# Two residual additions moved from TensorE to VectorE in a graph attention kernel

## The chip, the cores and the metric

The kernel runs on one core of one Trainium2 chip. The metric is the device time of one execution in microseconds (us); lower is better. Three runs of the kernel before the change are given.

## The reference, cut to what matters

One graph attention layer with four heads, a residual and a layer norm. `x` is 4096x512, `adj` is 4096x4096, `W` is 512x2048, `a` is 4x1024x1, all in float32.

```python
ht = (h @ W).reshape(N, N_HEADS, N_HIDDEN).transpose(1, 0, 2)
src = jnp.einsum('hnd,hd->hn', ht, a[:, :N_HIDDEN, 0])
dst = jnp.einsum('hnd,hd->hn', ht, a[:, N_HIDDEN:, 0])
e = jax.nn.leaky_relu(src[:, :, None] + dst[:, None, :], SLOPE) + adj_mat[None]
att = jax.nn.softmax(e, axis=-1)
h_prime = jnp.einsum('hij,hjd->hid', att, ht).mean(axis=0)
x = _layernorm(x + h_prime, axis=-1)
```

The entries of `adj` reach 1e9 while the scores beside them are small. Where the largest entry of a row leads by enough, the softmax of that row is one-hot: the row's output is then `layernorm(x[i] + x[col] @ mean_over_heads(W))`, with `col` the column of the largest entry. The kernel computes that (`leading_rows`), tests at the end that every row leads by enough, and has a second function (`general`) for the rows that don't. With these inputs the second is not entered.

## The kernel before, in words

The 4096 rows are 32 blocks of 128. The main loop of `leading_rows` runs over t from 0 to 31, and the order of every engine's instructions is the order in which this Python code is written: nothing is rearranged, so each engine has one fixed list. At step t the code writes:

- SP: the load of `adj` of block t+5 (2 MB; six buffers, so the load waits until VectorE has finished with block t-1).
- VectorE: `segment_maxima(t)` reads the 128x4096 tile of `adj` and takes maxima of its segments (line 212; in one piece in blocks 12 to 19, in two halves before and after), `find_segment(t)` finds the row's largest segment (lines 222 and 224), and `find_column(t-2)` finds the largest entry in that segment of block t-2, which GpSimd has fetched again (lines 264 and 270). In blocks 5 to 19 `find_column` stands behind `find_segment`, from block 20 on between the halves of `segment_maxima`.
- GpSimd (POOL): from VectorE's index, the fetch of the segment (`lead`, line 230), and from the column the fetch of the row of `x` (`y`, line 255), both indirect DMAs of one row for each partition.
- TensorE (PE), for block t-3: `spread` (one matmul `px`, line 331), `turn` (four transposes of `y`, line 284), `residual` (the block of x, which lies in `hold`, times the identity, into the sum `o` in PSUM, line 296; a float32 matmul is two records in the profile), `from_table` (three bf16 matmuls, line 343) and `products` (`y` times the mean of W over the heads, four float32 matmuls in eight records, line 303).
- ScalarE (ACT): `off` and `pick` from `px` (lines 333 and 335), the copy of the transposes to SBUF (`yt`, line 286), then for block t-4 `row_norm` (the sum of squares of x, which reads `hold`, line 347) and `parked_stats` (lines 372 and 374: it copies the sum `o` from PSUM over x in `hold` and takes mean and variance), and for block t-11 `finish` (line 391), and `clear_rows` for the next gather (line 245).

`root` (line 377) takes the square roots of the deviations of four blocks at once, 12 to 15 at t = 19 and 16 to 19 at t = 23. `add_sums` (line 360) exists already for two of the last blocks: VectorE adds the sum in PSUM and x.

```python
def residual(ib):
    start = ib not in o_ps
    if start:
        o_ps[ib] = psum.tile([P, D], F32, name="o")
    nc.tensor.matmul(o_ps[ib], ident, hold[:, ib, :], start=start, stop=False)

def add_sums(ib, out):
    nc.vector.tensor_add(out, o_ps[ib], hold[:, ib, :])
    o_ps[ib] = out
```

Of the kernel before, what the change touches and what calls it, by code (L numbers as in the profile page):

```python
# [27 lines left out]
LAST = 4  # L28
SKIP = 8192
TABLED = range(1, 28)  # L30


@with_exitstack
# [40 lines left out]
def leading_rows(ctx, tc, x, adj, W, a, out, ident, leads, any_bad):  # L74
# [17 lines left out]
    BEHIND = LATE - Q  # L92
# [3 lines left out]
    hold = landing.tile([P, NB, D], F32, name="hold")  # L96
# [22 lines left out]
    def pieces(ib):  # L119
        return PIECES if ib == NB - 1 else 2 if ib >= LATE else 1  # L120

    def load_adj(ib):
        if 0 <= ib < NB:
            t = adj_t[ib] = adj_pool.tile([P, N], F32, name="adj_t")
            n = pieces(ib)
            for k in range(n):
                rows_of = adj_rows[ib - 1] if ib else adj[:P, :]
                nc.sync.dma_start(t[:, ts(k, N // n)], rows_of[:, ts(k, N // n)])

    def load_x(lo, n):  # L130
        if lo == 0:
            nc.sync.dma_start(hold[:, 0, :], x[:P, :])
            lo, n = 1, n - 1
        if n:
            nc.sync.dma_start(hold[:, ds(lo, n), :], x_rows[:, ds(lo - 1, n), :])
# [59 lines left out]
    def span_of(ib):  # L195
        return next(k for k, (_, lo, hi) in enumerate(spans) if lo <= ib < hi)
# [4 lines left out]
    def segment_maxima(ib, lo, hi):  # L201

        if ib == NB - 1:
            for k in range(lo, hi):
                nc.vector.max(out=best[:, k, :], in_=adj_t[ib][:, ts(k, N // PIECES)])
            return
        e = spans[span_of(ib)][0]
        if lo == 0:
            seg_of[ib] = small.tile([P, N // e], F32, name=f"seg{e}", bufs=2)
        n = max(pieces(ib), 1 if ib in WHOLE else 2)  # L210
        for k in range(lo * n // PIECES, hi * n // PIECES):
            nc.vector.tensor_reduce(  # L212
                seg_of[ib][:, ts(k, N // e // n)],
                adj_t[ib][:, ts(k, N // n)].rearrange("p (s e) -> p s e", e=e), axis=AX.X, op=OP.max,
            )

    def find_segment(ib):
        if ib == NB - 1:
            nc.vector.max(out=top[:, ib, :], in_=best)
            return  # L220
        seg = seg_of.pop(ib)
        nc.vector.max(out=top[:, ib, :], in_=seg)  # L222
        at = at_of[ib] = small.tile([P, 8], U32, name="at")
        nc.vector.max_index(at, top[:, ib, :], seg)  # L224
        row = small.tile([P, 1], U32, name="row")
        nc.gpsimd.tensor_tensor(row, at[:, 0:1], first[:, ib : ib + 1], op=OP.add)  # L226
        k = span_of(ib)
        e = spans[k][0]
        lead = lead_pool.tile([P, e], F32, name=f"lead{e}", bufs=LEADS[k])
        nc.gpsimd.indirect_dma_start(  # L230
            out=lead, out_offset=None, in_=adj_segs[e],
            in_offset=bass.IndirectOffsetOnAxis(ap=row[:, :1], axis=0),
        )
        lead_of[ib] = lead
        start = at_of[ib] = small.tile([P, 1], U32, name="start")
        if ib in TABLED:
            away = small.tile([P, 1], F32, name="away")
            nc.gpsimd.tensor_scalar(away, at[:, 0:1], float(P // e), float(SKIP), op0=OP.is_lt, op1=OP.mult)
            nc.gpsimd.tensor_scalar(start, at[:, 0:1], float(e), away, op0=OP.mult, op1=OP.add)
        else:  # L240
            nc.gpsimd.tensor_tensor(start, at[:, 0:1], width[:, k : k + 1], op=OP.mult)
# [5 lines left out]
    def gather_rows(ib, col):  # L247
        if ib not in TABLED:
            y = y_t[ib] = y_pool.tile([P, D], F32, name="y")
            nc.gpsimd.indirect_dma_start(  # L250
                out=y, out_offset=None, in_=x,
                in_offset=bass.IndirectOffsetOnAxis(ap=col[:, :1], axis=0),
            )
            return
        nc.gpsimd.indirect_dma_start(  # L255
            out=y_t[ib], out_offset=None, in_=x,
            in_offset=bass.IndirectOffsetOnAxis(ap=col[:, :1], axis=0),
            bounds_check=N - 1, oob_is_err=False,
        )
        low = low_of[ib] = small.tile([P, 1], BF16, name="low")  # L260
        nc.gpsimd.tensor_scalar(low, col, float(SKIP - 1), float(SKIP - 1), op0=OP.max, op1=OP.subtract)
# [4 lines left out]
    def find_column(ib):  # L266
        if ib < BEHIND:
            find_inner(ib)
        within = small.tile([P, 8], U32, name="within")
        nc.vector.max_index(within, top[:, ib, :], lead_of[ib])  # L270
        col = small.tile([P, 1], U32, name="col")
        nc.gpsimd.tensor_tensor(col, at_of.pop(ib), within[:, 0:1], op=OP.add)  # L272
        gather_rows(ib, col)
# [15 lines left out]
    def turn(ib):  # L289
        yt_of[ib] = turned_rows(y_t.pop(ib))  # L290
# [68 lines left out]
# [3 lines that stand above are left out]
# [8 lines left out]
    def parked_stats(ib):  # L370
        o, i = o_ps.pop(ib), slice(ib, ib + 1)
        nc.scalar.activation(hold[:, ib, :], o, AF.Identity, scale=-1.0 / D, accum_out=nm[:, i])  # L372
        sq = rows.tile([P, D], F32, name="sq")
        nc.scalar.activation(sq, hold[:, ib, :], AF.Square, bias=nm[:, i], scale=-float(D), accum_out=sd[:, i])  # L374
# [4 lines left out]
    def scales(i):  # L379
        nc.gpsimd.tensor_mul(nm[:, i], nm[:, i], sd[:, i])  # L380
        nc.gpsimd.tensor_scalar(sd[:, i], sd[:, i], -float(D), None, op0=OP.mult)
# [153 lines left out]
    COLUMN, PROJECT, STATS = 2, 3, 4  # L535
# [4 lines left out]
    def lag_of(hi):  # L540
        return hi - 1 + STATS + (3 if hi < BEHIND - 2 else 2)
# [4 lines left out]
    for t in range(NB):  # L546
        if t == NB // 2:
            tc.mark_branch_hint_location("general", engines=HINTED)
        if t in x_at:
            load_x(*x_at[t])  # L550
        if t + AHEAD == NB - 1:
            load_x(LATE, 2)
        load_adj(t + AHEAD)
        middle = PIECES if t in END else 1 if t == NB - 1 else 2
        segment_maxima(t, 0, middle)
        if t >= COLUMN and t not in END and t != COLUMN + 1:
            find_column(t - COLUMN)
            if t == lag_of(BEHIND) + 1:
                scales(slice(BEHIND - 2, BEHIND))
        if t not in END:  # L560
            segment_maxima(t, middle, PIECES)
        if t == NB - 1:
            for ib in (BEHIND, LATE + 2, BEHIND + 2):
                load_x(ib, 2)
        find_segment(t)
        if t in END:
            find_column(t - 1 if t <= COLUMN else t - COLUMN)
        if t + 1 in TABLED:
            clear_rows(t + 1)
        for lo, hi in FACTORS:  # L570
            if t == lag_of(hi):
                nc.vector.reciprocal(sd[:, lo:hi], sd[:, lo:hi])
                if hi < BEHIND:
                    scales(slice(lo, hi))
        if t < 2:
            mean_of_heads(t)
        elif t == 2:
            mean_of_heads(2)
            mean_of_heads(3)
            fill_table()  # L580
        if t == 0:
            square_sums_of_a()
        if 21 <= t < 24:
            head_norms(t - 21)
        ib = t - PROJECT
        if t == NB - 2:
            finish(BEHIND - 3)
            finish(BEHIND - 2)
        if t == NB - 1:
            row_norm(LATE)  # L590
            row_norm(LATE + 1)
            finish(BEHIND - 1)
            residual(LATE + 1)
        if ib >= 0:
            if ib in TABLED:
                spread(ib)
            turn(ib)
            if ib > BEHIND:
                products(ib - 1, KB - 1, KB)
            if ib < BEHIND:  # L600
                residual(ib)
            if ib in TABLED:
                from_table(ib)
            products(ib, 0, KB if ib < BEHIND else KB - 1)
            if ib == 0:
                split_table()
        for _ in range(squares_at.get(t, 0)):
            square_sum_of_w(squares.pop(0))
        if t >= BEHIND + STATS:
            put_by(t - STATS)  # L610
        elif t >= STATS:
            row_norm(t - STATS)
            parked_stats(t - STATS)
        for lo, hi in FACTORS:
            if t == hi - 1 + STATS:
                root(slice(lo, hi))
        for done in FINISHED.get(t, ()):
            finish(done)
# [253 lines left out]
```

## Time and profile before

| | |
|---|---|
| median of three runs | 233.9 us (233.88 to 234.27) |
| profiled execution | 233.53 us, of which the span from the first to the last instruction is 232.0 us |
| PE busy | 197.6 us (85% of the span) |
| DVE (VectorE) busy | 189.6 us (82%) |
| ACT (ScalarE) busy | 153.2 us (66%) |
| POOL (GpSimd) busy | 111.5 us (48%) |
| DMA | 96.04 MB, mean 414 GB/s |

The busy shares are averages over stages with different limits. In the timeline a row is: start in us, duration in us, engine, line, operation, output tile from input tile, shapes, count, and in brackets the idle time of the engine before the row with what ended it. "Step t" below is the step of the main loop; because each engine has its own list, the engines are at different steps at one moment: TensorE's work of step t is on block t-3.

### The profile page before, as it was taken

How to read it: one execution, taken by the hardware profiler on the slowest of the kernel's cores; microseconds unless marked ns; L12 is line 12 of the kernel's file. 1: busy time of each engine (PE TensorE's matmuls, PEld its weight loads, DVE VectorE, ACT ScalarE, POOL GpSimd, SP SyncE). 2: the span in 40 equal slices, each digit the busy share in tenths (PEclk: the TensorE clock that was granted, in tenths of full speed). 3: DMA queues.
4: the chain of work that ended last, by engine and by line, in shares of the span. 5: the costliest groups of instructions: out<-in, count | busy, mean ns of one | idle time of the engine just before them, and what ended most of it. 6: DMA issues, size and time to landing. Idle time of an engine off the chain costs nothing.

```text
span 232.0 us, 2532 instructions
## 1 busy us (share of the span) xinstructions
PE 197.6 (85%) x604; PEld 95.5 (41%) x614; DVE 189.6 (82%) x296; ACT 153.2 (66%) x378; POOL 111.5 (48%) x254
## 2 busy tenths in 40 slices
PE   0069988779099999997999899999999999999990
PEld 0033443334044444443444345454544444545460
DVE  0448289899879997999699959996999999967882
ACT  3003213588075987797998678878888877958872
POOL 4020414525554556355635665554565665637620
PEclk9999999999859999999999999999999999999997
DMA  6999999999999999999999999999999999999995
GB/s 221 426 435 428 433 421 437 425 431 411 440 429 422 420 437 427 429 421 434 418 433 430 417 435 429 419 430 431 426 432 415 419 425 416 419 416 419 420 374 207
DMA packets 13379, 96.04 MB, mean 414 GB/s; under 512 B 2148, under 2 KB 2596, under 8 KB 7984
## 3 DMA queue, kind: packets, MB, share of 16 engines
q1 hardware_dynamic: 9792, 88.08, 90.0%
q0 software_dynamic: 3552, 7.73, 8.5%
q8 instruction: 6, 0.10, 0.2%
q14 instruction: 13, 0.11, 0.1%
q10 hardware_dynamic: 16, 0.02, 0.0%
HBM read 88.51 MB, written 8.39 MB: 418 GB/s over the span
## 4 chain that ended last, share of the span: by engine, by line
DMA 44%; PE 30%; DVE 19%; ACT 2%; issue 1%; POOL 1%; DVEq 0%; POOLq 0%; ACTq 0%
DMA adj_t<-in_adj_dram 39%; PE o L303 19%; DVE seg L212 15%; DMA y<-in_x_dram,col 4%; PE o L296 3%; PE o L343 3%; PE tp L284 3%; PE o L400 2%; DVE at L224 1%; DVE top L222 1%; DMA a_rows<-in_L_gnn_a_dram 1%; DVE inner L264 1%; POOL lead L230 0%; PE o L396 0%; ACT sq L368 0%
## 5 line engine op out<-in xcount | busy, mean ns | idle before, releaser
L212 DVE TENSOR_REDUCE seg<-adj_t 128x128 f32<-128x2048 f32 (+4 forms) x54 | 138.9, 2589 | 27.4 <-DMA adj_t<-in_adj_dram 27.4
L303 PE MATMUL o<-w_sum,yt 128*128 128x512 f32 x248 | 113.5, 598 | 1.1 <-ACT yt L286 0.8
L303 PEld LDWEIGHTS o<-w_sum,yt 128*128 128x128 f32 x248 | 46.8, 192 | 49.0 <-issue 42.0
L230 POOL DMA_INDIRECT lead<-in_adj_dram,row x31 | 32.5, 1050 | 14.5 <-POOL row L226 14.5
L255 POOL DMA_INDIRECT y<-in_x_dram,col x27 | 29.1, 1077 | 12.1 <-POOL col L272 6.1
L226 POOL TENSOR_TENSOR row<-at,first 128x1 uint32<-128x1 uint32 x31 | 5.8, 188 | 60.0 <-DVE at L224 43.6
L284 PE MATMUL tp<-ident,y 128*128 128x128 f32 x128 | 22.9, 302 | 12.0 <-DMA y<-in_x_dram,col 11.9
L286 ACT COPY yt<-tp 128x512 f32<-128x512 f32 x33 | 19.0, 576 | 14.2 <-PE tp L284 13.9
L451 PE MATMUL o<-hold,ident 128*128 128x512 f32 x32 | 16.4, 671 | 14.0 <-DMA hold<-in_L_gnn_W_dram 14.0
L284 PEld LDWEIGHTS tp<-ident,y 128*128 128x128 f32 x128 | 18.3, 210 | 23.9 <-issue 17.8
L296 PE MATMUL o<-hold,ident 128*128 128x512 f32 x50 | 26.5, 612 | 0.0
L333 ACT ACTIVATE off<-px,minus 128x128 f32<-128x128 f32 x27 | 9.9, 366 | 19.9 <-PE px L331 19.8
L343 PE MATMUL o<-z,pick 128*128 128x512 bf16 x72 | 20.4, 386 | 1.1 <-ACT pick L335 0.8
L347 ACT ACTIVATE sq<-hold 128x512 f32<-128x512 f32 x32 | 20.0, 625 | 0.0
L391 ACT ACTIVATE hold<-hold,nm,sd 128x512 f32<-128x512 f32 x24 | 18.8, 801 | 0.0
L374 ACT ACTIVATE sq<-hold,nm 128x512 f32<-128x512 f32 x24 | 17.3, 722 | 0.8
L452 ACT ACTIVATE w_sum<-o 128x512 f32<-128x512 f32 x4 | 2.4, 597 | 22.5 <-PE o L451 22.5
L245 ACT COPY y<-zero 128x512 f32<-128x512 f32 x27 | 16.3, 603 | 0.0
L451 PEld LDWEIGHTS o<-hold,ident 128*128 128x128 f32 x32 | 6.7, 216 | 22.9 <-issue 21.6
L343 PEld LDWEIGHTS <-pick 128*128 128x128 bf16 x81 | 7.8, 100 | 19.9 <-issue 10.5
L372 ACT ACTIVATE hold<-o 128x512 f32<-128x512 f32 x24 | 14.3, 597 | 0.8
L222 DVE MAX8 top<-seg 128x8 f32<-128x256 f32 (+2 forms) x31 | 11.3, 366 | 1.1
(117 smaller groups left out, 190.3 us busy)
## 6 DMA issues: line engine op xcount, KB each, us to landing
adj_t<-in_adj_dram SPq DMA_DIRECT2D x28, 2048.0 KB, 33.1
adj_t<-in_adj_dram SPq DMA_DIRECT2D x6, 1024.0 KB, 27.3
out_dram<-hold SPq DMA_DIRECT2D x12, 512.0 KB, 10.1
hold<-in_x_dram SPq DMA_DIRECT2D x5, 1024.0 KB, 33.0
hold<-in_L_gnn_W_dram SPq DMA_DIRECT2D x2, 2048.0 KB, 16.5
hold<-in_x_dram SPq DMA_DIRECT2D x4, 512.0 KB, 12.7
adj_t<-in_adj_dram SPq DMA_DIRECT2D x4, 512.0 KB, 18.6
out_dram<-hold SPq DMA_DIRECT2D x4, 256.0 KB, 2.8
```

The costliest lines, as they stand in the source:

```text
L212: nc.vector.tensor_reduce(seg_of[ib][:, ts(k, N // e // n)], adj_t[ib][:, ts(k, N // n)].rearrange("p (s e) -> p s e", e=e), axis=AX.X, op ...
L230: nc.gpsimd.indirect_dma_start(out=lead, out_offset=None, in_=adj_segs[e], in_offset=bass.IndirectOffsetOnAxis(ap=row[:, :1], axis=0),)
L255: nc.gpsimd.indirect_dma_start(out=y_t[ib], out_offset=None, in_=x, in_offset=bass.IndirectOffsetOnAxis(ap=col[:, :1], axis=0), bounds_che ...
L284: nc.tensor.transpose(tp[:, kb, :], y[:, ds(kb, P, KB)], ident)
L286: nc.scalar.copy(yt, tp)
L296: nc.tensor.matmul(o_ps[ib], ident, hold[:, ib, :], start=start, stop=False)
L303: nc.tensor.matmul(o_ps[ib], yt_of[ib][:, kb, :], w_sum[:, kb, :], start=(start and kb == 0), stop=(kb == KB - 1),)
L343: nc.tensor.matmul(o_ps[ib], pick, z[k], start=(start and k == 0), stop=False)
L347: nc.scalar.activation(sq, hold[:, ib, :], AF.Square, accum_out=xx[:, ib : ib + 1])
L374: nc.scalar.activation(sq, hold[:, ib, :], AF.Square, bias=nm[:, i], scale=-float(D), accum_out=sd[:, i])
L391: nc.scalar.activation(hold[:, ib, :], o, AF.Identity, bias=nm[:, i], scale=sd[:, i])
L451: nc.tensor.matmul(o, ident, hold[:, w_at + kb * H + h, :], start=(h == 0), stop=(h == H - 1))
```

## The change

For blocks 15 and 18 `residual` is left out, so the sum in PSUM holds the products alone. VectorE adds x to it with `add_sums` and writes the result to `hold`, over x. The addition of block ib stands in step ib+5 (20 and 23), after the order for the next load of `adj` and ahead of VectorE's first instruction on the `adj` of that step. `parked_stats` of the two blocks moves one step later, behind `row_norm` of the next block, and reads `hold` instead of PSUM; `root` of blocks 12 to 15 moves from step 19 to step 20.

```diff
+ADDED = (15, 18)
...
         load_adj(t + AHEAD)
         middle = PIECES if t in END else 1 if t == NB - 1 else 2
+        if t - STATS - 1 in ADDED:
+            add_sums(t - STATS - 1, hold[:, t - STATS - 1, :])
         segment_maxima(t, 0, middle)
...
-            if ib < BEHIND:
+            if ib < BEHIND and ib not in ADDED:
                 residual(ib)
...
             row_norm(t - STATS)
-            parked_stats(t - STATS)
+            for ib in (t - STATS - 1, t - STATS):
+                if (ib in ADDED) == (ib < t - STATS):
+                    parked_stats(ib)
         for lo, hi in FACTORS:
-            if t == hi - 1 + STATS:
+            if t == hi - 1 + STATS + (hi - 1 in ADDED):
                 root(slice(lo, hi))
```

In the lists of the built programs the lines after the first change are one or more higher. Numbers behind names are buffers; `adj_t_959` is the `adj` of block 20, `o_1173` the sum of block 15, `o_1346` that of block 18.

VectorE at the step from 19 to 20, before:

```order
L264 MAX inner_140<-lead16_1083 128x8
L270 MAX_INDEX within_1204<-top_139,lead16_1083 128x8
L212 TENSOR_REDUCE seg32_1246<-adj_t_959 128x64
L264 MAX inner_140<-lead32_1139 128x8
L270 MAX_INDEX within_1249<-top_139,lead32_1139 128x8
```

and after, with the addition as the third row:

```order
L265 MAX inner_140<-lead16_1083 128x8
L271 MAX_INDEX within_1203<-top_139,lead16_1083 128x8
L361 TENSOR_TENSOR hold_68<-o_1173,hold_68 128x512
L213 TENSOR_REDUCE seg32_1242<-adj_t_959 128x64
L265 MAX inner_140<-lead32_1139 128x8
L271 MAX_INDEX within_1245<-top_139,lead32_1139 128x8
```

The addition stands ahead of the first half of block 20's maxima and of the search for the column of block 18 behind it.

ScalarE in the same steps, before: `off`, `pick`, `yt` of block 16, `row_norm` and `parked_stats` of block 15, `root`, `finish`, then the start of step 20.

```order
L333 ACTIVATE off_1217<-px_1215,minus_133 128x128
L335 ACTIVATE pick_1219<-off_1217 128x128
L286 COPY yt_1226<-tp_1221 128x512
L347 ACTIVATE sq_1237,xx_143<-hold_68 128x512
L372 ACTIVATE hold_68,nm_144<-o_1173 128x512
L374 ACTIVATE sq_1240,sd_145<-hold_68,nm_144 128x512
L377 ACTIVATE sd_145<-sd_145,eps_127 128x4
L391 ACTIVATE hold_68<-hold_68,nm_144,sd_145 128x512
```

And after, from the same `row_norm` of block 15 to `root`, between which step 20 now begins (the third row clears a buffer for a gather):

```order
L348 ACTIVATE sq_1236,xx_143<-hold_68 128x512
L392 ACTIVATE hold_68<-hold_68,nm_144,sd_145 128x512
L246 COPY y_1266<-zero_129 128x512
L334 ACTIVATE off_1270<-px_1268,minus_133 128x128
L336 ACTIVATE pick_1272<-off_1270 128x128
L287 COPY yt_1279<-tp_1274 128x512
L348 ACTIVATE sq_1290,xx_143<-hold_68 128x512
L373 ACTIVATE hold_68,nm_144<-hold_68 128x512
L375 ACTIVATE sq_1293,sd_145<-hold_68,nm_144 128x512
L373 ACTIVATE hold_68,nm_144<-o_1227 128x512
L375 ACTIVATE sq_1296,sd_145<-hold_68,nm_144 128x512
L378 ACTIVATE sd_145<-sd_145,eps_127 128x4
```

`row_norm` of block 15 (line 347, now 348) keeps its place, behind the copy of block 16's transposes. It reads the x that the addition overwrites.

TensorE at block 18, before:

```order
L331 LDWEIGHTS low_1256
L331 MATMUL px_1333<-ident_b_135,low_1256 128x128
L284 MATMUL tp_1339<-ident_60,y_1099 128x128 x4
L296 MATMUL o_1346<-hold_68,ident_60 128x512
L343 LDWEIGHTS pick_1337
L343 MATMUL o_1346<-z0_149,pick_1337 128x512
```

and after:

```order
L332 LDWEIGHTS low_1252
L332 MATMUL px_1333<-ident_b_135,low_1252 128x128
L285 MATMUL tp_1339<-ident_60,y_1099 128x128 x4
L344 LDWEIGHTS pick_1337
L344 MATMUL o_1346<-z0_149,pick_1337 128x512
```

The residual's matmul is gone; nothing else on TensorE moves, and GpSimd's and SP's lists are the same row by row.

## The prediction

> **What bounds the kernel now.** I read the span and clock first, then the busy time of the stretches around the change, then VectorE's rows there with what ended each wait, then the chain that ended last, and from there the rows of the engines that VectorE would wait for.
>
> ```profile
> core 0: 232.0 us, clock 0.980
> 158.53:206.64 48.11, 47.51 (x155) 23.37 (x157) 46.98 (x71) 39.33 (x94) 27.43 (x63) 1.00 1.01 422
> ```
>
> The second row is the stretch from the maxima of block 23 to the last loop step: TensorE is busy 47.51 of 48.11 us and VectorE 46.98. Neither has room there; a delay of either ahead of it is not worked off inside it. VectorE's waits lie before:
>
> ```profile
> 136.39 0.17 DVE L270 FIND_INDEX8 within<-top,lead 128x8 uint32<-128x16 f32 x1
> 139.07 2.29 DVE L212 TENSOR_REDUCE seg<-adj_t 128x64 f32<-128x2048 f32 x1 [2.51 <-DMA adj_t<-in_adj_dram]
> 144.79 2.29 DVE L212 TENSOR_REDUCE seg<-adj_t 128x64 f32<-128x2048 f32 x1 [0.26 <-DMA adj_t<-in_adj_dram]
> 150.66 2.29 DVE L212 TENSOR_REDUCE seg<-adj_t 128x64 f32<-128x2048 f32 x1 [0.29 <-DMA adj_t<-in_adj_dram]
> 158.53 2.29 DVE L212 TENSOR_REDUCE seg<-adj_t 128x64 f32<-128x2048 f32 x1 [2.00 <-DMA adj_t<-in_adj_dram]
> ```
>
> These are blocks 20 to 23. VectorE is free from 136.56 to 139.07 and from 156.53 to 158.53: the waits into which the two additions are put. What they need is on other engines, whose rows are these, TensorE at blocks 15 to 19 first:
>
> ```profile
> 137.26 0.72 PE L284 MATMUL tp<-ident,y 128*128 128x128 f32 x4 [0.43 <-DMA y<-in_x_dram,col]
> 142.76 0.22 PE L331 MATMUL px<-ident_b,low 128*128 128x128 bf16 x1
> 142.81 0.70 PE L284 MATMUL tp<-ident,y 128*128 128x128 f32 x4
> 148.91 0.72 PE L284 MATMUL tp<-ident,y 128*128 128x128 f32 x4 [0.40 <-DMA y<-in_x_dram,col]
> 155.01 0.70 PE L284 MATMUL tp<-ident,y 128*128 128x128 f32 x4
> 155.71 0.86 PE o L296 x2
> 160.54 0.70 PE L284 MATMUL tp<-ident,y 128*128 128x128 f32 x4
> 143.63 0.57 ACT L286 COPY yt<-tp 128x512 f32<-128x512 f32 x1
> 144.09 0.63 ACT L347 ACTIVATE sq<-hold 128x512 f32<-128x512 f32 x1
> 144.62 0.19 ACT L347 ACTIVATION_READ_ACCUMULATOR sq<-hold 128x1 f32 x1
> 161.82 0.63 ACT L347 ACTIVATE sq<-hold 128x512 f32<-128x512 f32 x1
> ```
>
> Block 15 begins on TensorE at 137.26 and its products end at 142.76, where the next block's `px` starts: 3.7 us after VectorE wants to go on. Block 18's products end at about 160.5, when VectorE is at block 23 since 158.53. And the addition overwrites x, which ScalarE's `row_norm` reads first: 144.09 to 144.81 for block 15, from 161.82 for block 18 (three blocks of `row_norm` later).
>
> **The change, part by part.** *Removed:* two float32 residual matmuls, 0.86 us each (the row of the chain). Block 15's gain ends at 148.91, where TensorE waits for `y` of block 17: nothing of it is left there, only a longer wait than 0.40. Block 18's would shorten the chain by 0.86, if TensorE waited for nothing behind it.
>
> *Added:* two additions of 128x512 from PSUM and SBUF, a form that the last blocks have:
>
> ```profile
> 223.36 0.69 DVE L360 TENSOR_TENSOR hold<-o,hold 128x512 f32<-128x512 f32 x1
> ```
>
> I take 0.65 until the next start, as records overlap a little.
>
> *First wait (block 15).* `row_norm` of block 15 follows `yt` of block 16 on ScalarE, so it needs block 16's transposes, and these need block 16's `y`. Gathers by GpSimd and their landing:
>
> ```profile
> 134.04 1.07 POOL L255 DMA_INDIRECT y<-in_x_dram,col  x1 [0.44 <-POOL col L272]
> 142.58 1.11 POOL L255 DMA_INDIRECT y<-in_x_dram,col  x1 [0.68 <-ACT y L245]
> 148.29 1.09 POOL L255 DMA_INDIRECT y<-in_x_dram,col  x1 [0.68 <-ACT y L245]
> 154.16 1.09 POOL L255 DMA_INDIRECT y<-in_x_dram,col  x1 [0.67 <-ACT y L245]
> 162.03 1.09 POOL L255 DMA_INDIRECT y<-in_x_dram,col  x1 [0.68 <-ACT yt L286]
> 139.45 9.32 DMA y<-in_x_dram,col
> DMA to landing us min/median/max: 8.4/8.4/8.4
> DMA to landing us min/median/max: 7.4/7.4/7.4
> DMA to landing us min/median/max: 6.1/8.0/9.3
> adj_t<-in_adj_dram SPq DMA_DIRECT2D x28, 2048.0 KB, 33.1
> ```
>
> The issues are those of blocks 16, 18, 19, 20 and 21; 9.32 is block 17's time to landing, and 8.4 that of each of the other five; 7.4 is that of a gather at 173, then all from 120 to the end; the last row is for the loads of `adj`. Block 16's `y` is there at 142.44, and at 142.58 the transposes can start (as block 17's, at 148.91, 0.14 after landing at 148.77): 0.23 earlier than at 142.81. So `row_norm` ends at 144.6 instead of 144.81 (bounds: 143.95 if the whole 0.86 came through, 144.85 if nothing). The addition runs then, and block 20's maxima start at 145.2 instead of 139.07: **+6.1 us**.
>
> *What queues behind it.* Block 20's maxima, the columns of blocks 18 and 19, and so their gathers. Block 18's gather goes to 148.7, lands at 157.1, and TensorE starts the block at 157.2 instead of 155.01. VectorE's work of step 20 takes 5.46 us (139.07 to 144.79 less the wait of 0.26): step 21 starts at 150.65 without a wait, since its `adj` landed at 144.79. Block 19's gather stands 3.50 behind that start (148.29 less 144.79): 154.15, lands at 162.55, transposes at 162.7. TensorE itself is ready at 157.2 + 5.53 - 0.86 = 161.9 (5.53 is 155.01 to 160.54), so this wait swallows the second residual's gain too.
>
> *Second wait (block 18).* Steps 21 and 22 of VectorE take 5.58 (to 150.66 less 0.29) and 5.87 (to 156.53): free at 162.1. `row_norm` of block 18 ends 2.0 us after block 19's transposes start (142.81 to 144.81 for the pair before): 164.7. A wait of 2.6, the addition, and block 23's maxima start at 165.35 instead of 158.53: **+6.8 us**. The `adj` that landed in time is no help, and the loads behind stay ahead: each was ordered about 33 us before it landed, so an order 6 us later still finds the queue filled.
>
> *To the end.* VectorE has no wait from there to 206.64, so all 6.8 stay. The end:
>
> ```profile
> 206.44 0.20 DVE L219 MAX8 top<-best 128x8 f32<-128x32 f32 x1
> 208.46 0.09 DVE L270 MATCH_VALUE_LOAD within<-top,lead 128x8 f32 x1 [1.83 <-DMA lead<-in_adj_dram,row]
> 208.69 0.09 DVE L278 MATCH_VALUE_LOAD col<-top,adj_t 128x8 f32 x1
> 221.28 0.72 PE L284 MATMUL tp<-ident,y 128*128 128x128 f32 x4 [0.26 <-DMA y<-in_x_dram,col]
> 222.38 0.48 ACT yt L286
> ```
>
> The one wait, 1.83, is for a fetch that VectorE's own index orders, so it moves along. TensorE's last block waited for its `y` already (0.26), and `y` comes 6.8 later; its transposes ended at 222.0, and ScalarE copied them at 222.38, so at most 0.4 is slack. 6.4 to 6.8; I take 6.5.
>
> *Moved:* `parked_stats` and, for block 15, `root` go to steps 20 and 23. The two rows are ScalarE's start with them and the next work:
>
> ```profile
> 144.85 0.60 ACT L372 ACTIVATE hold<-o 128x512 f32<-128x512 f32 x1
> 146.62 0.80 ACT L391 ACTIVATE hold<-hold,nm,sd 128x512 f32<-128x512 f32 x1
> ```
>
> That is up to 1.77 us more in each step. It is hidden by TensorE's new waits (2.2 us ahead of block 18, 3.5 ahead of block 21, below). Reading `hold` instead of PSUM costs nothing to speak of (0.63 for line 347 from `hold`, 0.60 here).
>
> The sum for the profiled execution is 233.53 + 6.5 = 240.0; the median of the runs is 0.37 higher, so 240.3 after rounding. Removing 1.7 us of TensorE's work gives nothing, because a late VectorE decides. With every gather between 7.4 and 9.3 us the second `row_norm` moves by about 1 us either way: 239.1 to 241.5 for this case.
>
> [...] The row at 208.69 shows the order kept: the search over `adj` (line 278) had its inputs at 206.64 and started only after line 270, which waited 1.83. [...]
>
> **The rivals.**
>
> *Faster: the additions find their inputs in time.* Then block 18's residual comes off the chain: 233.9 - 0.86 = 233.0. It needs `row_norm` done by 138.4 and 157.9; the rows have 144.81 and about 162.5. Only a shift of several us between the engines decides for it: 4%. Another 3% for a mixture that ends within 0.2%.
>
> *Only the products count, not `row_norm`.* First start at about 142.7 (+3.6); the second, with block 18 hardly late on TensorE, at about 160.3 (+1.8): 235.3. The list shows the read ahead of the overwrite, so 4%.
>
> *The second wait vanishes*, because VectorE is so late that block 18 is done: 162.1 + 0.65 against 158.53 is +4.2, with the tail 237.8. It needs the gathers of blocks 18 and 19 2.6 us shorter together; the late rows have 6.1, at a time with fewer requests: 12%.
>
> *TensorE slows.* It ends block 20 at 168.2 + 5.53 = 173.8 (gather at 156.2 + 3.5, landing 168.1) and gets block 21's `y` at 162.03 + 6.8 + 8.4 = 177.2: 3.5 us of nearly nothing. A short and a long gap of before, and the granted clock behind the long one (0.50, ahead of the last two numbers):
>
> ```profile
> 107.25 0.72 PE L284 MATMUL tp<-ident,y 128*128 128x128 f32 x4 [1.32 <-DMA y<-in_x_dram,col]
> 63.42 1.10 PE L284 MATMUL tp<-ident,y 128*128 128x128 f32 x4 [5.76 <-DMA y<-in_x_dram,col]
> 64.00:66.00 2.00, 2.00 (x5) 0.80 (x4) 0.31 (x5) 1.44 (x4) 1.31 (x3) 0.50 1.00 427
> 71.72 0.70 PE L284 MATMUL tp<-ident,y 128*128 128x128 f32 x4
> ```
>
> After 5.76 us the granted clock was 0.50 and the block took 8.30 instead of 5.53. With 2.8 us more TensorE is about 8.5 behind and decides the end: 242.2. Behind the gap of 1.32 the block took its usual time. 3.5 lies between the two: 14%. [...]
>
> **How the numbers follow.** My forecast has 60%, the cold clock 14%, one wait 12%, products alone 4%, faster 4%, same 3%, and 3% something slower still. The range goes from the one-wait case to the cold clock, 237.5 to 242.4. A run of this kernel tells about 0.2% (0.5 us) from no change: faster 4%, within it 3%, slower 93%.
>
> **What the profile after would show.** VectorE idle about 8.0 us ahead of the first addition and about 2.6 ahead of the second, both ended by line 348 of ScalarE; block 20's maxima at 145.2, block 23's at 165.3, with no wait for `adj` behind; 46 records of the residual instead of 50; TensorE waiting some 2 us ahead of block 18 and 3.5 ahead of block 21, and its last `y` at about 228. I am wrong if the additions' waits end with TensorE or with `adj`, if gathers get much faster, or if the end moves less than block 23's start.

## The result and the profile after

The changed kernel takes 241.06 us (median of four executions, 239.68 to 241.55) against 233.89: a ratio of 1.0292, with an interval of 1.0262 to 1.0322. The profiled execution takes 239.68 us, 6.15 more than the one before (233.53). The range on record, 237.5 to 242.4, holds both.

VectorE's rows around the two additions, from the timeline after, and the end of ScalarE's `row_norm` ahead of each (all lines are one higher than before, behind the main loop's start more):

```profile
core 0: 238.1 us, clock 0.982
136.39 0.17 DVE L271 FIND_INDEX8 within<-top,lead 128x8 uint32<-128x16 f32 x1
144.47 0.69 DVE L361 TENSOR_TENSOR hold<-o,hold 128x512 f32<-128x512 f32 x1 [7.91 <-ACT sq L348]
145.08 2.28 DVE L213 TENSOR_REDUCE seg<-adj_t 128x64 f32<-128x2048 f32 x1
161.53 0.23 DVE L485 TENSOR_TENSOR n<-o,w 128x4 f32<-128x4 f32 x2
164.24 0.69 DVE L361 TENSOR_TENSOR hold<-o,hold 128x512 f32<-128x512 f32 x1 [2.48 <-ACT sq L348]
164.85 2.28 DVE L213 TENSOR_REDUCE seg<-adj_t 128x64 f32<-128x2048 f32 x1
144.25 0.19 ACT L348 ACTIVATION_READ_ACCUMULATOR sq<-hold 128x1 f32 x1
164.02 0.19 ACT L348 ACTIVATION_READ_ACCUMULATOR sq<-hold 128x1 f32 x1
```

Up to 136.56 nothing has moved. Then VectorE stands for 7.91 us ahead of the first addition and 2.48 ahead of the second, both times until ScalarE's `row_norm` (line 348) has read the x that the addition overwrites: it ends at 144.44 and 164.21, the additions start at 144.47 and 164.24. VectorE's four waits for `adj`, 5.06 us together before, are gone: it comes to each of these tiles over 5 us after the time at which the tile had landed before.

TensorE at blocks 17 to 21, and its last block, then the busy times of a stretch and a wait of VectorE in it:

```profile
149.63 0.72 PE L285 MATMUL tp<-ident,y 128*128 128x128 f32 x4 [1.44 <-DMA y<-in_x_dram,col]
156.06 0.38 PE L477 MATMUL o<-each,ones 8*128 8x8 f32 x2 [0.64 <-DVE each L474]
156.91 0.72 PE L285 MATMUL tp<-ident,y 128*128 128x128 f32 x4 [0.30 <-DMA y<-in_x_dram,col]
162.25 0.72 PE L285 MATMUL tp<-ident,y 128*128 128x128 f32 x4 [0.19 <-DMA y<-in_x_dram,col]
168.08 0.72 PE L285 MATMUL tp<-ident,y 128*128 128x128 f32 x4
176.72 0.72 PE L285 MATMUL tp<-ident,y 128*128 128x128 f32 x4 [2.93 <-DMA y<-in_x_dram,col]
227.70 0.75 PE L285 MATMUL tp<-ident,y 128*128 128x128 f32 x4
164.85:213.50 48.65, 45.21 (x148) 21.59 (x147) 46.99 (x72) 35.47 (x85) 26.96 (x60) 1.00 1.02 420
209.59 0.09 DVE L271 MATCH_VALUE_LOAD within<-top,lead 128x8 f32 x1 [0.63 <-DMA lead<-in_adj_dram,row]
```

Both residuals are gone, and TensorE waits for `y` instead: 1.44 ahead of block 17, where 0.40 stood, and 2.93 ahead of block 21. The stretch from 164.85 runs from block 23's maxima to the end of the loop, as it was shown of before: it starts 6.3 us later, VectorE is as busy as then (46.99 us against 46.98), and TensorE has gaps now. It is 0.54 longer (48.65 against 48.11), for VectorE now waits 0.63 in it for a segment that GpSimd fetches.

### The profile page after: what moved, and what is told of

The parts are those of the page before. It is cut to its first block, busy times and chain, and to the rows that moved or that the text cites. A ratio compares the mean times of both kernels' runs of the same rounds, so it can differ in the third digit from the quotient of the medians.

```text
span 238.1 us, 2537 instructions
## 1 busy us (share of the span) xinstructions
PE 198.2 (83%) x610; PEld 94.5 (40%) x610; DVE 190.8 (80%) x298; ACT 153.0 (64%) x378; POOL 111.5 (47%) x254
## 4 chain that ended last, share of the span: by engine, by line
DMA 56%; DVE 24%; POOL 6%; issue 5%; PE 5%; ACT 3%; POOLq 0%; DVEq 0%; ACTq 0%
DMA adj_t<-in_adj_dram 38%; DVE seg L213 19%; DMA y<-in_x_dram,col 14%; DMA out_dram<-hold 3%; POOL lead L231 3%; PE o L304 2%; DVE at L225 2%; PE o L401 1%; DVE top L223 1%; PE tp L285 1%; POOL y L256 1%; DMA a_rows<-in_L_gnn_a_dram 1%; DVE within L271 1%; ACT sq L348 1%; ACT hold L373 1%
## 5 line engine op out<-in xcount | busy, mean ns | idle before, releaser
L452 PE MATMUL o<-hold,ident 128*128 128x512 f32 x32 | 16.4, 671 | 14.0 <-DMA hold<-in_L_gnn_W_dram 14.0
L297 PE MATMUL o<-hold,ident 128*128 128x512 f32 x46 | 24.4, 614 | 0.0
L344 PE MATMUL o<-z,pick 128*128 128x512 bf16 x81 | 22.6, 389 | 0.8 <-ACT pick L336 0.7
L373 ACT ACTIVATE hold<-o 128x512 f32<-128x512 f32 x22 | 13.1, 595 | 0.6
L273 POOL TENSOR_TENSOR col<-start,within 128x1 uint32<-128x1 uint32 x31 | 5.8, 188 | 16.4 <-DVE within L271 15.0
```

The source lines that it names most:

```text
L344: nc.tensor.matmul(o_ps[ib], pick, z[k], start=(start and k == 0), stop=False)
L452: nc.tensor.matmul(o, ident, hold[:, w_at + kb * H + h, :], start=(h == 0), stop=(h == H - 1))
```

## The experiments

All start from the changed kernel.

**One block at a time.** Is it the two waits, and how do they add up?

```diff
-ADDED = (15, 18)
+ADDED = (15,)        # only15
+ADDED = (18,)        # only18
```

> Block 15 alone is added by VectorE; block 18 keeps its residual on TensorE. My account: block 20's maxima start about 6.0 us late as in the changed kernel, but at step 23 VectorE meets no second addition, and the wait of 2.0 for adj there and the small ones before absorb part: block 23's maxima start near 161.8 instead of 158.5, +3.2. End +2.8 to +3.2: 236.9 us (236.4 to 237.5). TensorE's wait ahead of block 21 is then about 1 us, so its clock stays full. If one long wait alone were the whole loss, this would take 241; if the first wait were wholly absorbed, 234.

Measured: 237.18 us, ratio 1.0145 (1.0111 to 1.0179). VectorE in its timeline:

```profile
144.81 0.69 DVE L361 TENSOR_TENSOR hold<-o,hold 128x512 f32<-128x512 f32 x1 [7.83 <-ACT sq L348]
162.03 2.27 DVE L213 TENSOR_REDUCE seg<-adj_t 128x64 f32<-128x2048 f32 x1
```

The same first wait, and block 23's maxima at 162.03 without a wait: 3.5 us late, where 3.2 was expected. Block 20's maxima had started 6.35 late (145.42 against 139.07); of the 2.85 regained since, 2.55 are the three waits for `adj` that are gone. TensorE does not wait ahead of block 21, where about 1 us was expected.

> Block 18 alone is added by VectorE; block 15 keeps its residual on TensorE. My account: VectorE comes to the addition at 156.5, row_norm of block 18 ends near 162.0, block 23's maxima start near 162.7 instead of 158.5: +4.1, end 237.8 us (237.2 to 238.5) with a full clock. TensorE then waits some 3 us ahead of block 21, so executions in which its clock drops there would come out up to 2 us longer. If the two waits simply added up, only15 and this one together would give the 7.2 of the changed kernel; by my account they give 7.3, the second partly standing in the shadow of the first.

Measured: 238.48 us, ratio 1.022 (1.0174 to 1.0267).

```profile
162.31 0.69 DVE L361 TENSOR_TENSOR hold<-o,hold 128x512 f32<-128x512 f32 x1 [5.84 <-ACT sq L348]
162.92 2.27 DVE L213 TENSOR_REDUCE seg<-adj_t 128x64 f32<-128x2048 f32 x1
174.63 1.10 PE L285 MATMUL tp<-ident,y 128*128 128x128 f32 x4 [3.13 <-DMA y<-in_x_dram,col]
```

Alone, the second addition waits 5.84 us, not 2.48: with the first one ahead of it VectorE comes later and waits less. At block 23 the two kernels are 3.50 and 4.39 us late, 7.89 together, and the changed kernel only 6.32: the waits do not simply add up. By the medians they cost 3.1 and 4.4 (against 234.12), 7.4 together, and the changed kernel 7.2, or 6.2 in the repetition below, where its executions spread too far to show the difference.

**What the additions wait for.** The sum goes back to PSUM, so nothing that ScalarE reads is overwritten:

```diff
-            add_sums(t - STATS - 1, hold[:, t - STATS - 1, :])
+            add_sums(t - STATS - 1, o_ps[t - STATS - 1])
```

> Both additions stand where the changed kernel has them, but write the sum back to PSUM instead of over x, so row_norm no longer has to come first; only the products do. My account: the first addition starts at about 142.2 (not 144.5), the second at about 160.2 (not 164.2), block 23's maxima about 2.3 late, end +1.9 to +2.3: 236.0 us (235.4 to 236.7). Rival: the waits are for the products and the profile names row_norm only because it ends last; then this takes the same 241 as the changed kernel.

Measured: 236.33 us, ratio 1.0106 (1.0088 to 1.0124).

```profile
142.36 0.70 DVE L361 TENSOR_TENSOR o<-o,hold 128x512 f32<-128x512 f32 x1 [5.73 <-PE o L304]
160.68 0.70 DVE L361 TENSOR_TENSOR o<-o,hold 128x512 f32<-128x512 f32 x1 [0.98 <-PE o L304]
```

Now TensorE's products end both waits, at 142.36 and 160.68 (142.2 and 160.2 expected). So the read by `row_norm` is a cause of its own, and about two thirds of the loss; the last third is that the products themselves are not ready when VectorE comes.

**What the removed work is worth.** This kernel leaves x out of the sums of blocks 15 and 18 altogether:

```diff
-        if t - STATS - 1 in ADDED:
-            add_sums(t - STATS - 1, hold[:, t - STATS - 1, :])
```

> Leaves out the addition of x in blocks 15 and 18: neither TensorE's residual nor VectorE's addition; the statistics stay one step later, and read PSUM. My account: VectorE sets the end, so 1.7 us less of TensorE's work gives 0 to 0.4: 233.7 us (233.4 to 234.1). Rival: TensorE is the bound from 149 on as the chain of waits has it, and the time falls by one residual or two, to 233.0 or 232.2.

Measured: 233.75 us, ratio 0.9988 (0.9975 to 1.0002). With the statistics where the change puts them, 1.7 us less of TensorE's work and no addition at all are worth 0.1%, and the interval takes in no change: the change had at most 0.6 us to win, whatever VectorE's side had cost.

**The same additions where their inputs are there.** Block 15 at step 21, block 18 at step 24, with statistics, `root` and reciprocals moved along.

```diff
-ADDED = (15, 18)
+ADDED = {15: 6, 18: 6}
...
-        if t - STATS - 1 in ADDED:
-            add_sums(t - STATS - 1, hold[:, t - STATS - 1, :])
+        for ib, lag in ADDED.items():
+            if t == ib + lag:
+                add_sums(ib, hold[:, ib, :])
...
+            if t == ib + ADDED.get(ib, STATS):
+                parked_stats(ib)
```

> The same two additions where their inputs are there: block 15 at the start of step 21 (row_norm ended at about 144.8, VectorE comes at 144.5), block 18 at the start of step 24 (row_norm ended at 162.6, VectorE comes at 164.2). Statistics and root move along. My account: no long wait; the first addition is absorbed by the waits for adj of blocks 22 and 23, the second puts 0.65 on VectorE's full stretch, TensorE loses one residual there: 234.3 us (233.7 to 234.9). If it is the work on VectorE or the later statistics that costs, and not the place, it takes 237 or more.

Measured: 234.29 us, ratio 1.002 (1.0004 to 1.0036).

```profile
144.56 0.69 DVE L361 TENSOR_TENSOR hold<-o,hold 128x512 f32<-128x512 f32 x1
158.50 2.29 DVE L213 TENSOR_REDUCE seg<-adj_t 128x64 f32<-128x2048 f32 x1 [2.07 <-DMA adj_t<-in_adj_dram]
164.22 0.69 DVE L361 TENSOR_TENSOR hold<-o,hold 128x512 f32<-128x512 f32 x1
156.52 0.59 PE L344 MATMUL o<-z,pick 128*128 128x512 bf16 x2 [0.49 <-ACT pick L336]
162.37 0.82 PE L344 MATMUL o<-z,pick 128*128 128x512 bf16 x3 [0.38 <-ACT pick L336]
```

Neither addition has a wait in front. One step of place is worth 6.0 us against the repetition of the changed kernel (240.29, below), 6.8 against its first four executions; the additions themselves and the later statistics cost next to nothing. The two rows of TensorE show where block 18's 0.86 goes: without the residual in front, the matmuls with `pick` wait 0.49 for ScalarE, and the `pick` of block 19, which now stands behind block 15's statistics on ScalarE, comes 0.38 late.

**An addition that fits a wait.** One block whose `row_norm` is done when VectorE waits for `adj` of block 23; the addition is written at the end of step 22, so its statistics move by one step only.

```diff
-ADDED = (15, 18)
+ADDED = (17,)
...
-        if t - STATS - 1 in ADDED:
-            add_sums(t - STATS - 1, hold[:, t - STATS - 1, :])
         segment_maxima(t, 0, middle)
...
             head_norms(t - 21)
+        if t - STATS - 1 in ADDED:
+            add_sums(t - STATS - 1, hold[:, t - STATS - 1, :])
```

> One block only, 17, added by VectorE in the wait for adj of block 23 (156.5 to 158.5), with row_norm of block 17 done at 157.0 or, as TensorE is one residual ahead, at 156.2. Its statistics go one step later. My account: the addition fits into the wait, TensorE's chain is 0.86 shorter from 154 to 200, and the last blocks wait for y, which VectorE sets: 0 to 0.4 less, 233.7 us (233.4 to 234.1). If TensorE were the bound to the end, 233.0; if the addition doesn't fit, 234.5 or more.

Measured: 233.47 us (13 executions) against 234.09 (23): ratio 0.9976 (0.9967 to 0.9984). It beats both kernels, the one before by 0.24%: little, but the interval leaves no change out.

```profile
156.80 0.69 DVE L361 TENSOR_TENSOR hold<-o,hold 128x512 f32<-128x512 f32 x1 [0.31 <-ACT sq L348]
158.40 2.29 DVE L213 TENSOR_REDUCE seg<-adj_t 128x64 f32<-128x2048 f32 x1 [0.91 <-DMA adj_t<-in_adj_dram]
216.62 0.72 PE L285 MATMUL tp<-ident,y 128*128 128x128 f32 x4 [0.17 <-DMA y<-in_x_dram,col]
221.42 0.72 PE L285 MATMUL tp<-ident,y 128*128 128x128 f32 x4 [0.44 <-DMA y<-in_x_dram,col]
228.01 0.56 ACT L441 ACTIVATE hold<-o,nm,sd 128x256 f32<-128x256 f32 x1 [0.42 <-DVE nm L423]
```

The addition lies inside the wait, with 0.91 left over. Of the 0.86 that TensorE is spared, 0.25 is left at block 18 (154.76 against 155.01), because block 17's `y` came later; TensorE keeps this until its last two blocks wait for `y`, so even that stops at what VectorE sets. The profiled execution is the longest of the 13 (235.01 us), and its length comes from the very end: the last calculation, the last row, ends at 228.57, 0.08 earlier than before (228.65), yet the span ends 1.4 later (233.4 against 232.0). Behind it only stores of the results are left; the kernel's four stores of 256 KB took 4.7 us from order to landing there (median) and 2.8 before. So this profile shows that the addition fits, but not where the 0.6 us between the medians comes from.

**What spreads the executions.** The changed kernel again, and with three matmuls more in TensorE's wait ahead of block 21:

```diff
+            if ib == 21:
+                spare = psum.tile([P, KB, P], F32, name="tp", bufs=2)
+                for _ in range(3):
+                    nc.tensor.matmul(spare.rearrange("p k c -> p (k c)"), ident, hold[:, 0, :], start=True, stop=True)
             turn(ib)
```

> The changed kernel once more, unaltered, for more executions: 239.6 to 241.6 us each. What is asked: whether the longer ones have the lower mean granted clock, as the first four had (0.982 with 239.68, 0.971 with 241.55). If TensorE's clock drops ahead of block 21 in some executions only, the two go together; if something else spreads the times, they don't.

> The changed kernel with three more matmuls of 128x512 on TensorE (x of block 0 times the identity into a buffer that nobody reads), 0.86 us each, ahead of block 21's transposes, where TensorE waits 2.9 us. They fill 2.6 us of that wait. If a dropped clock behind that wait makes the usual execution longer than 239.7, all executions come to 239.6 to 240.2 with a granted clock of 0.98. If not, the median stays at 241.1, and if the matmuls push block 21 back it is higher.

Measured: `again` 240.29 us (239.91 to 240.59), ratio 1.0266 (1.0252 to 1.028); `warm` 240.4 (239.79 to 240.92), ratio 1.027 (1.0253 to 1.0287). No difference, so the expectation of `warm` failed: if the drop made the spread, all its executions should have lain at 239.6 to 240.2, and three of five lie above; nor did the median stay at 241.1, it is that of `again`. In its profiled execution the matmuls leave 0.54 us of the wait, the clock does not fall there, and it took 239.89. Nor is a drop at block 21 a sign of a long execution: the profiled one of `only18` has it (block 21's transposes above take 1.10 us instead of 0.72) and is the second shortest of its four (238.12 to 240.43). The mean granted clock doesn't decide it either. In the changed kernel's first four it falls as the time rises (0.982 with 239.68, 0.971 with 241.55), in `warm` roughly so (0.984 with 239.79, 0.972 with 240.63, 0.975 with 240.92), but all of `again` have 0.977 or 0.978. And the mean also counts a drop near 60 us, before the change (0.86 from 58 to 64 in the changed kernel's profile, 0.71 in that of `again`), and the end, where TensorE has nothing left to do (0.50 from 237 on in the changed kernel's).

Yet the profiled one of `again` did have the dropped clock, in the third row the granted clock ahead of the last two numbers:

```profile
177.01 1.10 PE L285 MATMUL tp<-ident,y 128*128 128x128 f32 x4 [3.17 <-DMA y<-in_x_dram,col]
183.92 0.70 PE L285 MATMUL tp<-ident,y 128*128 128x128 f32 x4
177.00:178.00 1.00, 0.99 (x5) 1.00 (x6) 1.00 (x1) 0.00 (x0) 0.95 (x1) 0.50 1.10 468
227.73 0.75 PE L285 MATMUL tp<-ident,y 128*128 128x128 f32 x4
```

Block 21 took 6.91 us there, 1.35 more than the 5.56 of the execution above, and the last block still started at 227.73 instead of 227.70, since its `y` came no earlier. Its end is 0.6 us later (240.28 against 239.68): its chain runs through TensorE from 204 on, the other's through the gathers of `y`. So the dropped clock may have cost these 0.6 us; that it makes the spread from 239.7 to 241.5 is not shown, and what does stays open. The stores behind the last calculation, which cost `fit17`'s profiled execution 1.4 us, are a candidate, but none of the three executions above 240.8 us was profiled.

## Why the prediction was right

| step of the prediction | forecast | measured |
|---|---|---|
| wait ahead of the first addition, ended by `row_norm` | 8.0 us | 7.91 |
| block 20's maxima | 145.2 | 145.08 |
| TensorE's wait ahead of block 18 | 2.2 us | 0.64 and 0.30 |
| TensorE at block 18 | 157.2 | 156.91 |
| at block 19, on its `y` | 162.7 | 162.25 |
| wait ahead of the second addition | 2.6 | 2.48 |
| block 23's maxima | 165.35 | 164.85 |
| wait ahead of block 21 | 3.5 | 2.93 |
| TensorE's last block | about 228 | 227.70 |
| profiled execution | 240.0 | 239.68 |
| median | 240.3 | 241.06, again 240.29 |

The working held at each place but one, TensorE's wait ahead of block 18. The decisive step was to ask not when VectorE is free but when the inputs are, and to include what the addition overwrites. `to_psum` shows that this last wait carries about two thirds of the loss; without it the sum would have been near the 235.3 of the second rival (the kernel made to do that took 236.33, since its maxima of block 23 started at 161.28, 2.75 late and not 1.8, and the tail gave nothing back).

Terms that were off, all small. The lateness at block 23 was 6.3 us, not 6.8: blocks 18 and 19 of TensorE came 0.3 and 0.45 earlier than forecast, and `row_norm` with them. From there all of it was to stay to the end of the loop, since VectorE would not wait. It did wait, the 0.63 at 209.59, and was 6.86 late at the end of the loop (213.30 against 206.44). The tail then gave back 0.7, where I had let 0.3 go: the wait of 1.83 behind the loop became 1.33, and the profiled execution ended 6.15 late. Half a microsecond too much and half too little cancelled, so that the sum came out within 0.4 is in part luck. So is the median of `again` to the hundredth, as the executions spread over more than a microsecond.

TensorE's wait ahead of block 18 was to be 2.2 us, and 0.94 came, 0.64 and 0.30. The working left block 17 where it was, at 148.91; it started at 149.63, 0.72 later, since its `y` landed 10.1 us after its order and not 9.3. I had also not named that VectorE's `each` (line 474) feeds a small matmul of TensorE ahead of block 18, for which TensorE stood the 0.64. Neither cost anything: block 18's `y` landed later still, and that set the start.

The rival of the dropped clock got the place right and the price wrong. I took 2.8 us for block 21 from the one drop of before and let it reach the end; `again` has 1.35 for the block and 0.6 at the end. And I gave it 14% for a gap of 3.5 us, an estimate from two gaps of before, 1.32 us without a drop and 5.76 with one. The clock fell in two of the profiled executions shown here with gaps of 3.1 to 3.2 (`only18`, `again`) and not in the one with 2.93, so 14% looks too low. By the times in the last section the length of the gap alone does not decide, and how often 3.5 us would have dropped the clock is not shown. That the low chance did no harm is due to the small price.

Removing TensorE's work was priced at nothing, and `no_x` bears it out within 0.3%.

## What to carry to other kernels

A wait of one engine is only room for work whose inputs are ready inside it: read the end of each producer in its own row, and count the reader of what is overwritten as a producer too. Between engines that run two or three blocks apart, a step in the code is not a moment in time; the same instruction one step later cost 0.2% instead of 2.9%. And behind a stall look for the next stretch without a wait: VectorE had none for 48 us, so nearly all that it lost before stayed to the end.

## What the runs showed of the hardware

The clock fell sooner and came back sooner than I had read from the profile of before. In `again` TensorE's last matmul ahead of the gap started at 173.62 and took 0.22; these are the stretches around the drop. A row has the stretch, its length, the busy time of TensorE, its weight loads, VectorE, ScalarE and GpSimd, then the granted clock, the DMA share and GB/s.

```profile
176.00:176.50 0.50, 0.00 (x0) 0.00 (x0) 0.50 (x2) 0.00 (x0) 0.16 (x1) 1.00 0.95 395
176.50:177.00 0.50, 0.00 (x0) 0.02 (x1) 0.50 (x1) 0.00 (x0) 0.03 (x1) 0.53 0.88 363
179.00:180.00 1.00, 0.82 (x2) 0.15 (x1) 1.00 (x1) 0.97 (x4) 0.34 (x1) 0.53 1.03 430
180.00:181.00 1.00, 1.00 (x4) 0.61 (x4) 0.97 (x2) 0.97 (x4) 0.93 (x2) 1.00 1.02 428
```

A granted clock of 0.53 in the half microsecond from 176.50 means full speed for 0.03 and half speed behind; 0.53 from 179 means half speed until 179.94. So the drop began 2.7 us after the last matmul and lasted 3.41 us.

In `only18` the last matmul ahead of the gap ended at 171.50; the first two rows below hold the start and the end of its drop. The next two hold those of the drop of before, behind a matmul that ended at 57.66. The last two are from the changed kernel's profile, around its gap of 2.93 from 173.79 to 176.72:

```profile
174.00:174.63 0.63, 0.00 (x0) 0.03 (x1) 0.63 (x1) 0.00 (x0) 0.19 (x1) 0.82 1.00 423
177.00:178.00 1.00, 0.78 (x3) 0.34 (x3) 1.00 (x1) 0.96 (x3) 0.63 (x1) 0.59 1.06 447
62.00:62.50 0.50, 0.00 (x0) 0.00 (x0) 0.50 (x1) 0.00 (x0) 0.24 (x1) 0.83 1.07 455
69.00:70.00 1.00, 1.00 (x4) 0.51 (x3) 1.00 (x1) 0.06 (x1) 0.00 (x0) 0.92 0.96 402
174.00:176.00 2.00, 0.00 (x0) 0.00 (x0) 1.93 (x5) 1.03 (x3) 1.28 (x2) 1.00 1.02 434
176.00:178.00 2.00, 1.28 (x6) 0.88 (x7) 2.00 (x1) 0.52 (x2) 1.41 (x3) 1.00 0.94 395
```

Read in the same way, the drop of `only18` began at 174.40, 2.9 us after the last matmul, and lasted 3.4 us; that of before began at 62.33, 4.7 us after the last matmul, and lasted 6.8 us. In the changed kernel the granted clock stayed at 1.00 through 2.93 us without a matmul, longer than the 2.7 and 2.9 us after which it had fallen in `again` and `only18`. So the length of the gap alone does not decide; what else does, these traces leave open.

The granted clock does not account for all of TensorE's speed either: from 10 to 30 us in the profile of before its rows say 1.00, yet the first 16 matmul records, from 13.62 on, take 9.26 us and the next 16, of the same form, take 7.13.
